# Smaller first and last pairs of node blocks, a fourth place for x, and later loads and statistics in a graph layer on one core

## The chip, the cores and the metric

The kernel runs on one core of one Trainium2 chip. The metric is the device time in microseconds of one execution. Beside the timed runs there is one profiled execution, from which all durations of single instructions come. The core's engines are named as in the profile: PE (matrix multiply; PEld its weight loads), DVE (vector), ACT (scalar and activations), POOL and SP (SP issues most of the transfers, ACT issues those of x). Each engine works through its own instructions in the order in which the program writes them, and waits for the other engines through semaphores.

## The reference

One layer of a graph network over 12,500 nodes of 128 numbers and 412,500 edges of 48 numbers, sorted by the node `dst` that they point to:

```python
h = jnp.maximum(_layernorm(x, axis=-1), 0.0)
agg = jax.ops.segment_sum(edge_attr_48, dst, num_segments=12500)
u = graph_globals[0]                       # the same row for all nodes
cat = jnp.concatenate([h, agg, u], axis=1) # 128 + 48 + 64
hid = jax.nn.relu(cat @ W1 + b1)           # 256
out = x + (hid @ W2 + b2)                  # 128
```

All numbers are float32 (node indices int32).

## The kernel before, in words

**Edges.** The edges are cut into 403 chunks of 1,024, and these into two halves, s = 0 and s = 1, which run side by side on two halves of PE's array. Six chunks of each half form a group (CG = 6), and there are NI = 34 groups. One step of the main loop works on one chunk of each half: `contract` (L321) multiplies eight tiles of edges of each by a one-hot matrix, `oh`, and sums over the group in PSUM (`ps`). A step makes 32 matmul records in the profile, since each float32 matmul leaves two. `onehot` (L311) builds `oh` on DVE one group ahead: half s = 0 at the first step of a group, half s = 1 at its third. `add` (L337) adds the sums of the finished group into `aggT`, once for each half, also at the first step of the next group. Edges lie in a ring of PF = 14 buffers of two chunks each; `next_edges` asks for the next buffer once `contract` is done with one.

**Nodes.** The nodes are cut into 24 blocks of 512 (R = 4 rows on each of 128 partitions), taken in pairs: pair k has one block of each half of the edges, because the sums of both halves grow side by side. 212 nodes in the middle form the last block. For a pair, `normalization` makes eight statistics on DVE (bn_stats, L459), a variance and scale (`variance`, `finish`), and eight normalized rows on ACT (L455). `transpose` (L471) turns a block on PE, and ACT copies it to `hT` (L474). `hidden_x` (L489) multiplies it by the upper part of W1 into `ph`, and adds b2 to x on DVE (`xb`, L485), which is the last use of the block of x. `hidden_sums` (L500) adds the product with `aggT`, and ACT evicts `ph` to `hid` (L508). `output` (L519) makes one row of the result, and `store` adds `xb` (L527) and writes it out through SP (L530).

**Order.** The main loop has 204 steps and three more. In each it writes `contract`, then what `plan` has for the step, the adds and one-hot, waiting stores, one or two parts of the running normalization (`next_part`), and then as many PE pieces of the nodes as a running credit of 0.72 a step allows. The list `pieces` gives each piece the step from which it may run and a price. The sums of pair k may run from the step at which its last group, `ready[k]`, is added; its x parts eight steps sooner. What is left after the last step is written behind it.

**Loads of x.** There are XBUFS = 3 places, each for a pair. `pop_piece` asks for the next pair (`load_x`) when `xb` of the oldest one has been written. The loads are issued by ACT, by `next_x`, at steps given in a list or, at the latest, ahead of the first statistics of that pair:

```python
        if not parts and begun < min(len(pairs), freed + XBUFS):
            normalization(begun)
            begun += 1
        if parts and (force or ...):
            while x_loads and x_loads[0][0] <= parts[0][0]:
                next_x()
            parts.pop(0)[2]()
```

Of the kernel before, what the change touches and what calls it, by code (L numbers as in the profile page):

```python
# [16 lines left out]
P = 128  # L17
# [4 lines left out]
def kernel(  # L22
# [61 lines left out]
    BN = R * P  # L84
    XBUFS = 3
    CL = 2
    PF = 14
    GSTEP = N * GE / E
    LEAST = int(-OFF[0] - SL - 64)


    NP = N // BN // 2
    MID = NP * BN
    NM = N - 2 * NP * BN
    END = MID + NM
    assert NM % R == 0 and NM < BN
    blocks = []
    for k in range(NP):
        blocks += [(k * BN, P), (END + k * BN, P)]
    blocks.append((MID, NM // R))  # L100
    pairs = [[2 * k, 2 * k + 1] for k in range(NP)] + [[2 * NP]]

# [10 lines left out]
    ready = [min(NI - 1, max(  # L113
        int(-(-(blocks[j][0] + BN + PAD + 1 - LEAST - BEGIN[s]) // GSTEP)) - 1
        for s, j in enumerate(pairs[k]))) for k in range(NP)]

# [77 lines left out]

    def rows_of(ap, a, m):

        return ap[a:a + m * R].rearrange("(p r) d -> p (r d)", p=m)

# [3 lines left out]
    def load_x(k):  # L202

        if k >= len(pairs):
            return
        xt = xp.tile([P, 2, R * D], F32, name="xt")

        def load(i, j):
            a, m = blocks[j]
            f = m - m % 16  # L210
            nc.scalar.dma_start(xt[:f, i], rows_of(x, a, f))
            if f < m:
                nc.scalar.dma_start(xt[f:m, i], rows_of(x, a + f * R, m - f))

        for i, j in enumerate(pairs[k]):
            xs[j] = xt[:, i].rearrange("p (r d) -> p r d", d=D)
            x_loads.append((k, lambda i=i, j=j: load(i, j)))

    def next_x():
        if x_loads:  # L220
            x_loads.pop(0)[1]()

# [58 lines left out]
    with nc.allow_non_contiguous_dma(reason="a few hundred numbers, once"):  # L281
# [7 lines left out]
        nc.gpsimd.dma_start(b2_sb, b2[None, :].to_broadcast([P, D]))  # L289

    for k in range(XBUFS):
        load_x(k)
# [132 lines left out]
    def normalization(k):  # L425

        js = pairs[k]
        m = blocks[js[0]][1]
        q = len(js) * R
        st = sp.tile([P, 2 * R, 6], F32, name="st", bufs=2)  # L430
        sc = sp.tile([P, 2 * R], F32, name="sc", bufs=2)
        sh = sp.tile([P, 2 * R], F32, name="sh", bufs=2)
        su = sp.tile([P, 2 * R], F32, name="su")

        def variance():

            me, qe, mo, qo = [st[:m, :q, i] for i in (1, 2, 4, 5)]
            di = sp.tile([P, 2 * R], F32, name="df2")
            va = sp.tile([P, 2 * R], F32, name="va")
            nc.vector.tensor_tensor(di[:m, :q], me, mo, OP.subtract)  # L440
            nc.vector.tensor_tensor(va[:m, :q], qe, qo, OP.add)
            nc.vector.tensor_tensor(su[:m, :q], me, mo, OP.add)
            nc.vector.tensor_tensor(di[:m, :q], di[:m, :q], di[:m, :q], OP.mult)
            nc.vector.scalar_tensor_tensor(va[:m, :q], di[:m, :q], D / 4.0, va[:m, :q], OP.mult, OP.add)  # L444
            nc.scalar.activation(sc[:m, :q], va[:m, :q], AF.Sqrt, bias=eps[:m], scale=1.0 / D)  # L445

        def finish():
            nc.vector.reciprocal(sc[:m, :q], sc[:m, :q])
            nc.vector.scalar_tensor_tensor(sh[:m, :q], su[:m, :q], -0.5, sc[:m, :q], OP.mult, OP.mult)

        def row(i, j, r):
            if r == 0:
                xns[j] = mp.tile([P, R, D], F32, name="xn")
            c = i * R + r
            nc.scalar.activation(xns[j][:m, r], xs[j][:m, r], AF.Relu, bias=sh[:m, c:c + 1], scale=sc[:m, c:c + 1])  # L455

        for i, j in enumerate(js):
            for r in range(R):
                parts.append((k, None, lambda i=i, j=j, r=r: nc.vector.bn_stats(st[:m, i * R + r, :], xs[j][:m, r, :])))  # L459
        parts.append((k, None, variance))  # L460
        parts.append((k, None, finish))
        for i, j in enumerate(js):
            for r in range(R):
                parts.append((k, j, lambda i=i, j=j, r=r: row(i, j, r)))

    def transpose(j):
        m = blocks[j][1]
        pt = pst.tile([P, R, P], F32, name="pt")
        xn = xns.pop(j)
        for r in range(R):  # L470
            nc.tensor.transpose(pt[:, r, :m], xn[:m, r], ident[:m, :m])  # L471

        hT = mp.tile([P, P, R], F32, name="hT", bufs=4)
        nc.scalar.copy(hT[:, :m], pt[:, :, :m].rearrange("d r p -> d p r"))  # L474
        hTs[j] = hT.rearrange("d p r -> d (p r)")

    phs = {}

    def hidden_x(k, a, j):

        m = blocks[j][1]
        if a == 0:
            hids[j] = mp.tile([P, NH, R, P], F32, name="hid", bufs=4)
            xb = mp.tile([P, R, D], F32, name="xb", bufs=3)
            nc.vector.tensor_tensor(xb[:m], xs[j][:m], b2_sb[:m, None, :].to_broadcast([m, R, D]), OP.add)  # L485
            xbs[j] = xb
        phs[j, a] = psh.tile([P, BN], F32, name="ph")
        for c in (0, HI):
            nc.tensor.matmul(phs[j, a][c:c + HI, :R * m], w1h[:, a * P + c:a * P + c + HI], hTs[j][:, :R * m],  # L489
                             start=True, stop=False, skip_group_check=True)  # L490

    def hidden_sums(k, a):

        js = pairs[k]
        if len(js) == 2:
            for s, j in enumerate(js):
                at = blocks[j][0] + shift[s]
                h = slice(s * HI, s * HI + DE)
                for c in (0, HI):
                    nc.tensor.matmul(phs[j, a][c:c + HI], w1a[h, a * P + c:a * P + c + HI], aggT[h, at:at + BN],  # L500
                                     start=False, stop=True, skip_group_check=True)
# [4 lines left out]
        for j in js:  # L506
            m = blocks[j][1]
            nc.scalar.activation(hids[j][:, a, :, :m], phs.pop((j, a))[:, :R * m].rearrange("h (p r) -> h r p", r=R),  # L508
                                 AF.Relu, bias=bias[:, a:a + 1])

    def output(j, r):

        m = blocks[j][1]
        if r == 0:
            pos[j] = pso.tile([P, R, D], F32, name="po")
        for a in range(NH):
            for c in range(0, m, HI):
                k = min(m, c + HI)
                nc.tensor.matmul(pos[j][c:k, r], hids[j][:, a, r, c:k], w2[:, a], start=(a == 0), stop=(a == NH - 1),  # L519
                                 skip_group_check=True)  # L520
        if r == R - 1:
            late.append(j)

    def store(j):
        a0, m = blocks[j]
        ot = mp.tile([P, R, D], F32, name="ot")
        nc.vector.tensor_tensor(ot[:m], pos.pop(j)[:m], xbs.pop(j)[:m], OP.add)  # L527
        k = m - m % 16
        od = ot.rearrange("p r d -> p (r d)")
        nc.sync.dma_start(rows_of(out, a0, k), od[:k])  # L530
        if k < m:
            nc.sync.dma_start(rows_of(out, a0 + k * R, m - k), od[k:m])

# [10 lines left out]
    order = [j for js in pairs for j in js]  # L544
    pieces = [(8 + 3 * j, 0.9, lambda j=j: turn(j)) for j in order[:4]]
    for k, js in enumerate(pairs):
        at = CG * ((ready + [NI - 1])[k] + 1) + 2
        nxt = pairs[k + 2] if k + 2 < len(pairs) else []
        if len(js) == 1:
            pieces.append((at, 0.0, lambda: copy_middle(0)))  # L550
        parts_of = [(at - 8, 0.9, lambda k=k, a=a, j=j: hidden_x(k, a, j)) for a in range(NH) for j in js]
        sums = [(at, 0.9, lambda k=k, a=a: hidden_sums(k, a)) for a in range(NH)]
        m = len(js)
        pieces += parts_of[:m + 1] + sums[:1] + parts_of[m + 1:] + sums[1:]
        for s in range(2):
            if s < len(nxt):
                pieces.append((at, 0.9, lambda j=nxt[s]: turn(j)))
            if s < len(js):
                for r in range(R):
                    pieces.append((at, 0.45, lambda j=js[s], r=r: output(j, r)))  # L560
# [46 lines left out]
    first_nodes(1)  # L607
    next_x()
    next_x()


# [25 lines left out]
    at_step(NI - 1, 3, decide)  # L637
    for step in [4, 7] + list(range(12, CG * NI, 8)):
        at_step(0, step, next_x)

    credit = 0.0
    for step in range(CG * NI + 3):
# [3 lines left out]
        for f in plan.get(step, []):  # L646
            f()
        if k == 0:
            if i > 0:
# [21 lines left out]
    with tc.If(isbad >= 1):  # L671
# [63 lines left out]
        for k, js in enumerate(pairs):  # L735
# [12 lines left out]
            for j in js:  # L748
                for r in range(R):
                    output(j, r)  # L750
# [29 lines left out]
```

## Time and profile before

| | us |
|---|---|
| median of 3 timed runs | 374.79 (373.7 to 376.72) |
| the profiled execution | 374.44 |
| its span | 372.7 |
| busy: PE, PEld | 317.1, 248.3 |
| busy: DVE, ACT | 254.3, 110.0 |
| mean granted clock of PE | 0.943 |
| moved by DMA | 95.35 MB, mean 256 GB/s |

The page counts busy time by engine and cuts the span into 40 slices, in which digits give tenths. A row of a group ends with the idle time of the engine just ahead of that group and what ended most of it. The chain follows the work that ended last back to the start. "Issue" is time in which an engine waited for nothing that the profile shows. A matmul's end is modelled, so a busy PE is not always a fast one; the granted clock, in tenths of full speed on the page, stands beside it for that reason.

### The profile page before, as it was taken

To read this page: it belongs to the slowest core of one execution; us is meant where nothing else is said; L and a number is where in the kernel's file an instruction comes from. 1 tells how busy PE (TensorE), PEld (TensorE's weight loads), DVE (VectorE), ACT (ScalarE), POOL (GpSimd) and SP (SyncE) were. 2 spreads that over 40 slices of the span, in tenths; PEclk is the share of its full clock that TensorE was granted. 3 is DMA by queue.
4 is the path that set the end of the run, shared out by engine and by line. 5 is a ranking of instruction groups with operands and counts; after the bars stand their busy time and mean duration, and the time that the engine had idled before them with its cause. 6 is when DMAs were issued, how large, how long until landed. Compare 5 with 4: busy or idle time off the path is not lost.

```text
span 372.7 us, 17113 instructions
## 1 busy us (share of the span) xinstructions
PE 317.1 (85%) x7787; PEld 248.3 (67%) x7788; DVE 254.3 (68%) x413; ACT 110.0 (30%) x238; POOL 13.1 (4%) x44
## 2 busy tenths in 40 slices
PE   2667599797998998987998999699699898999982
PEld 1566476685785875774696687496397596696551
DVE  4677787876885885765767588695878594884420
ACT  3026406241242231260142341063122440341130
POOL 9400000000000000000000000000000000000000
PEclk9968899999998998899699999999799999999997
DMA  5999799999799899699588877999578979830111
GB/s 187 296 371 369 258 294 329 304 297 320 236 302 306 254 303 321 179 338 313 146 286 276 291 250 228 364 311 355 192 218 274 365 218 322 270 123 33 60 37 42
DMA packets 62812, 95.35 MB, mean 256 GB/s; under 512 B 4385, under 2 KB 55949, under 8 KB 62730
## 3 DMA queue, kind: packets, MB, share of 16 engines
q1 hardware_dynamic: 58864, 87.17, 71.7%
q10 hardware_dynamic: 3578, 6.50, 5.2%
q8 instruction: 63, 1.03, 1.2%
q0 software_dynamic: 288, 0.49, 0.5%
q14 instruction: 19, 0.16, 0.1%
HBM read 87.74 MB, written 6.40 MB: 253 GB/s over the span
## 4 chain that ended last, share of the span: by engine, by line
PE 48%; DVE 23%; DMA 20%; issue 4%; ACT 1%; SPq 1%; DVEq 1%; ACTq 0%
PE ps L321 23%; DMA xt<-in_x_dram 13%; DVE oh L311 13%; PE po L519 8%; DMA e<-in_edge_attr_dram 7%; PE ph L500 6%; PE ph L489 6%; PE pt L471 3%; DVE aggT L337 2%; DVE xb L485 2%; DVE st L459 2%; DVE ot L527 2%; ACT hid L508 1%; DVEq L332 0%; SPq L236 0%
## 5 line engine op out<-in xcount | busy, mean ns | idle before, releaser
L321 PEld LDWEIGHTS ps<-oh,e 128*48 128x48 f32 x6448 | 180.4, 131 | 70.6 <-issue 59.6
L321 PE MATMUL ps<-oh,e 128*48 128x44 f32 x6448 | 189.2, 223 | 16.8 <-issue 10.4
L311 DVE TENSOR_TENSOR oh<-iota,rel 128x2112 f32<-128x2112 f32 (+2 forms) x72 | 157.2, 2205 | 0.9
L508 ACT ACTIVATE hid<-ph,bias 128x512 f32<-128x512 f32 (+1 forms) x50 | 31.2, 671 | 98.2 <-PE ph L500 94.3
L519 PE MATMUL po<-w,hid 128*64 128x128 f32 (+1 forms) x784 | 58.1, 278 | 1.1 <-ACT hid L508 0.6
L489 PE MATMUL ph<-hT,w1h 128*64 128x512 f32 (+1 forms) x200 | 54.7, 624 | 0.8 <-ACT hid L508 0.8
L459 DVE BATCH_NORM_STATS2 st<-xt 128x6 f32<-128x128 f32 (+1 forms) x100 | 23.0, 281 | 46.2 <-DMA xt<-in_x_dram 46.2
L519 PEld LDWEIGHTS po<-w,hid 128*64 128x64 f32 (+1 forms) x784 | 43.4, 137 | 3.0 <-ACT hid L508 2.0
L337 DVE TENSOR_TENSOR aggT<-aggT,ps 48x199 f32 (+1 forms) x68 | 24.3, 357 | 28.8 <-PE ps L321 15.2
L500 PE MATMUL ph<-aggT,w1a 48*64 48x512 f32 x192 | 33.3, 659 | 9.8 <-DVE aggT L337 9.6
L455 ACT ACTIVATE xn<-xt,sh,sc 128x128 f32<-128x128 f32 (+1 forms) x100 | 40.4, 482 | 3.0 <-DMA e<-in_edge_attr_dram 1.5
L474 ACT COPY hT<-pt 128x512 f32<-128x512 f32 (+1 forms) x25 | 14.3, 573 | 45.6 <-PE pt L471 45.6
L527 DVE TENSOR_TENSOR ot<-po,xb 128x512 f32<-128x512 f32 (+1 forms) x25 | 17.3, 691 | 14.0 <-PE po L519 13.4
L471 PE MATMUL pt<-ident,xn 128*128 128x128 f32 (+1 forms) x100 | 17.9, 297 | 5.9 <-ACT xn L455 4.1
L445 ACT ACTIVATE sc<-va,eps 128x8 f32<-128x8 f32 (+1 forms) x13 | 3.9, 300 | 60.0 <-DVE va L444 60.0
L500 PEld LDWEIGHTS ph<-aggT,w1a 48*64 48x64 f32 x192 | 6.9, 135 | 16.1 <-DVE aggT L337 13.3
L471 PEld LDWEIGHTS pt<-ident,xn 128*128 128x128 f32 (+1 forms) x100 | 11.1, 146 | 9.1 <-ACT xn L455 5.1
L485 DVE TENSOR_TENSOR xb<-xt,b_sb 128x512 f32<-128x512 f32 (+1 forms) x25 | 16.3, 682 | 0.0
L489 PEld LDWEIGHTS ph<-hT,w1h 128*64 128x64 f32 x200 | 11.5, 142 | 3.1 <-ACT hid L508 1.7
L387 PE MATMUL pt<-ident,df 108*128 108x108 f32 (+2 forms) x36 | 6.6, 313 | 7.3 <-DVE df L366 7.3
L379 ACT COPY rel<-pt 128x216 f32<-128x216 f32 (+2 forms) x9 | 4.3, 473 | 27.1 <-PE pt L387 27.1
L395 ACT ACTIVATE far<-df,bounds 108x1024 f32<-108x1024 f32 (+2 forms) x10 | 11.5, 1147 | 0.2
(77 smaller groups left out, 63.5 us busy)
## 6 DMA issues: line engine op xcount, KB each, us to landing
e<-in_edge_attr_dram SPq DMA_DIRECT2D x200, 384.0 KB
xt<-in_x_dram ACTq DMA_DIRECT2D x24, 256.0 KB
out_dram<-ot SPq DMA_DIRECT2D x24, 256.0 KB
di<-in_dst_dram SPq DMA_DIRECT2D x6, 216.0 KB
e<-in_edge_attr_dram SPq DMA_DIRECT2D x2, 192.0 KB
di<-in_dst_dram SPq DMA_DIRECT2D x2, 108.0 KB
e<-in_edge_attr_dram SPq DMA_DIRECT2D x1, 159.0 KB
w1h<-in_L_gnn_W_dram POOLq DMA_DIRECT2D x1, 128.0 KB, 6.8
```

The lines of the kernel that those rows point to most:

```text
L311: nc.vector.tensor_tensor(hots[g][:, k0 * T:(k0 + n) * T], iota[:, None, :].to_broadcast([P, n * T, W]), r[:, :, None].to_broadcast([P, n ...
L321: nc.tensor.matmul(ps[s * HI:s * HI + DE, o:o + W], edges[c][0][:, t * DE:(t + 1) * DE], hots[g][:, k * T + t, :], start=(k == 0 and t == ...
L337: nc.vector.tensor_tensor(to, to, acc[i % len(acc)][h, :wg], OP.add)
L455: nc.scalar.activation(xns[j][:m, r], xs[j][:m, r], AF.Relu, bias=sh[:m, c:c + 1], scale=sc[:m, c:c + 1])
L459: parts.append((k, None, lambda i=i, j=j, r=r: nc.vector.bn_stats(st[:m, i * R + r, :], xs[j][:m, r, :])))
L471: nc.tensor.transpose(pt[:, r, :m], xn[:m, r], ident[:m, :m])
L485: nc.vector.tensor_tensor(xb[:m], xs[j][:m], b2_sb[:m, None, :].to_broadcast([m, R, D]), OP.add)
L489: nc.tensor.matmul(phs[j, a][c:c + HI, :R * m], w1h[:, a * P + c:a * P + c + HI], hTs[j][:, :R * m], start=True, stop=False, skip_group_ch ...
L500: nc.tensor.matmul(phs[j, a][c:c + HI], w1a[h, a * P + c:a * P + c + HI], aggT[h, at:at + BN], start=False, stop=True, skip_group_check=True)
L508: nc.scalar.activation(hids[j][:, a, :, :m], phs.pop((j, a))[:, :R * m].rearrange("h (p r) -> h r p", r=R), AF.Relu, bias=bias[:, a:a + 1])
L519: nc.tensor.matmul(pos[j][c:k, r], hids[j][:, a, r, c:k], w2[:, a], start=(a == 0), stop=(a == NH - 1), skip_group_check=True)
L527: nc.vector.tensor_tensor(ot[:m], pos.pop(j)[:m], xbs.pop(j)[:m], OP.add)
```

## The change

- The blocks get sizes of their own. The first two pairs and the last two have blocks of 256 nodes (two rows on each partition), the ten between have 512. There are 14 pairs and the middle, for 12 and the middle before. The sums of a pair, its x part, transposes, statistics and stores follow its size, and so do the prices of its pieces; `ready` too.
- There are four places for x, and 13 edge buffers.
- A load of x remembers the step at which its place came free. `next_x(4)` runs at every third step and issues at most one half of a pair, no sooner than four steps after that. Four halves are issued ahead of the loop.
- The statistics of a pair begin when both halves were issued and the last one at least eight steps ago. A forced part, which a transpose asks for, doesn't wait for this.
- The first four transposes stand at steps 9, 10, 14 and 15 for 8, 11, 14 and 17 before; the last two of them come behind the x parts of pair 0.

```diff
-    XBUFS = 3
+    XBUFS = 4
-    PF = 14
+    PF = 13
-    NP = N // BN // 2
-    MID = NP * BN
-    NM = N - 2 * NP * BN
+    sizes = [2, 2] + [R] * (N // BN // 2 - 2) + [2, 2]
+    NP = len(sizes)
+    MID = sum(sizes) * P
+    NM = N - 2 * MID
...
-    for k in range(NP):
-        blocks += [(k * BN, P), (END + k * BN, P)]
-    blocks.append((MID, NM // R))
+    for k, r in enumerate(sizes):
+        a = sum(sizes[:k]) * P
+        blocks += [(a, P, r), (END + a, P, r)]
+    blocks.append((MID, NM // R, R))
...
-            x_loads.append((k, lambda i=i, j=j: load(i, j)))
-
-    def next_x():
-        if x_loads:
-            x_loads.pop(0)[1]()
+            x_loads.append((k, lambda i=i, j=j: load(i, j), step))
+
+    came = {}
+
+    def next_x(late=0):
+
+        if x_loads and x_loads[0][2] <= step - late:
+            k, load, _ = x_loads.pop(0)
+            load()
+            came[k] = step
...
+    step = -4
     for k in range(XBUFS):
         load_x(k)
...
-    pieces = [(8 + 3 * j, 0.9, lambda j=j: turn(j)) for j in order[:4]]
+    early = [(at, 0.45, lambda j=j: turn(j)) for at, j in zip((9, 10, 14, 15), order)]
+    pieces = early[:2]
...
+        us = 0.9 * blocks[js[0]][2] / R
...
-        pieces += parts_of[:m + 1] + sums[:1] + parts_of[m + 1:] + sums[1:]
+        pieces += parts_of[:m + 1] + (early[2:] if k == 0 else []) + sums[:1] + parts_of[m + 1:] + sums[1:]
...
-        if not parts and begun < min(len(pairs), freed + XBUFS):
+        if not parts and begun < len(pairs) and (force or (
+                begun in came and not any(q == begun for q, _, _ in x_loads) and came[begun] <= step - 8)):
+            while x_loads and x_loads[0][0] <= begun:
+                next_x()
             normalization(begun)
             begun += 1
...
-            while x_loads and x_loads[0][0] <= parts[0][0]:
-                next_x()
             parts.pop(0)[2]()
...
-    next_x()
-    next_x()
+    for _ in range(4):
+        next_x()
...
-    for step in [4, 7] + list(range(12, CG * NI, 8)):
-        at_step(0, step, next_x)
...
             f()
+        if step % 3 == 2:
+            next_x(4)
         if k == 0:
...
+    step += 99
     while pieces:
         pop_piece()
```

More of the change, by code (lines that the diff above doesn't have):

```diff
@@ L113 @@
     ready = [min(NI - 1, max(
-        int(-(-(blocks[j][0] + BN + PAD + 1 - LEAST - BEGIN[s]) // GSTEP)) - 1
+        int(-(-(blocks[j][0] + blocks[j][2] * P + PAD + 1 - LEAST - BEGIN[s]) // GSTEP)) - 1
         for s, j in enumerate(pairs[k]))) for k in range(NP)]
@@ L193, in load_dst, with rows_of @@
         return di
-    def rows_of(ap, a, m):
-        return ap[a:a + m * R].rearrange("(p r) d -> p (r d)", p=m)
+    def rows_of(ap, a, m, r):
+        return ap[a:a + m * r].rearrange("(p r) d -> p (r d)", p=m)
     xs, xns, xbs, hTs, hids, pos = {}, {}, {}, {}, {}, {}
@@ L208, in load @@
         def load(i, j):
-            a, m = blocks[j]
+            a, m, r = blocks[j]
             f = m - m % 16
-            nc.scalar.dma_start(xt[:f, i], rows_of(x, a, f))
+            nc.scalar.dma_start(xt[:f, i, :r * D], rows_of(x, a, f, r))
             if f < m:
-                nc.scalar.dma_start(xt[f:m, i], rows_of(x, a + f * R, m - f))
+                nc.scalar.dma_start(xt[f:m, i, :r * D], rows_of(x, a + f * r, m - f, r))
         for i, j in enumerate(pairs[k]):
             xs[j] = xt[:, i].rearrange("p (r d) -> p r d", d=D)
-            x_loads.append((k, lambda i=i, j=j: load(i, j)))
-    def next_x():
-        if x_loads:
-            x_loads.pop(0)[1]()
+            x_loads.append((k, lambda i=i, j=j: load(i, j), step))
[5 more added lines that the diff above has]
+            came[k] = step
     first = const.tile([1, NG], I32)
@@ L427, in normalization @@
         js = pairs[k]
-        m = blocks[js[0]][1]
-        q = len(js) * R
+        _, m, nr = blocks[js[0]]
+        q = len(js) * nr
         st = sp.tile([P, 2 * R, 6], F32, name="st", bufs=2)
@@ L453, in row @@
                 xns[j] = mp.tile([P, R, D], F32, name="xn")
-            c = i * R + r
+            c = i * nr + r
             nc.scalar.activation(xns[j][:m, r], xs[j][:m, r], AF.Relu, bias=sh[:m, c:c + 1], scale=sc[:m, c:c + 1])
         for i, j in enumerate(js):
-            for r in range(R):
-                parts.append((k, None, lambda i=i, j=j, r=r: nc.vector.bn_stats(st[:m, i * R + r, :], xs[j][:m, r, :])))
+            for r in range(nr):
+                parts.append((k, None, lambda i=i, j=j, r=r: nc.vector.bn_stats(st[:m, i * nr + r, :], xs[j][:m, r, :])))
         parts.append((k, None, variance))
@@ L462, in normalization @@
         for i, j in enumerate(js):
-            for r in range(R):
+            for r in range(nr):
                 parts.append((k, j, lambda i=i, j=j, r=r: row(i, j, r)))
     def transpose(j):
-        m = blocks[j][1]
+        _, m, nr = blocks[j]
         pt = pst.tile([P, R, P], F32, name="pt")
         xn = xns.pop(j)
-        for r in range(R):
+        for r in range(nr):
             nc.tensor.transpose(pt[:, r, :m], xn[:m, r], ident[:m, :m])
-        hT = mp.tile([P, P, R], F32, name="hT", bufs=4)
-        nc.scalar.copy(hT[:, :m], pt[:, :, :m].rearrange("d r p -> d p r"))
-        hTs[j] = hT.rearrange("d p r -> d (p r)")
+        hT = mp.tile([P, BN], F32, name="hT", bufs=4)
+        hTs[j] = hT[:, :m * nr]
+        nc.scalar.copy(hTs[j].rearrange("d (p r) -> d p r", r=nr), pt[:, :nr, :m].rearrange("d r p -> d p r"))
     phs = {}
     def hidden_x(k, a, j):
-        m = blocks[j][1]
+        _, m, nr = blocks[j]
         if a == 0:
@@ L484, in hidden_x @@
             xb = mp.tile([P, R, D], F32, name="xb", bufs=3)
-            nc.vector.tensor_tensor(xb[:m], xs[j][:m], b2_sb[:m, None, :].to_broadcast([m, R, D]), OP.add)
+            nc.vector.tensor_tensor(xb[:m, :nr], xs[j][:m, :nr], b2_sb[:m, None, :].to_broadcast([m, nr, D]), OP.add)
             xbs[j] = xb
@@ L488, in hidden_x @@
         for c in (0, HI):
-            nc.tensor.matmul(phs[j, a][c:c + HI, :R * m], w1h[:, a * P + c:a * P + c + HI], hTs[j][:, :R * m],
+            nc.tensor.matmul(phs[j, a][c:c + HI, :nr * m], w1h[:, a * P + c:a * P + c + HI], hTs[j],
                              start=True, stop=False, skip_group_check=True)
@@ L497, in hidden_sums @@
                 at = blocks[j][0] + shift[s]
+                n = blocks[j][2] * P
                 h = slice(s * HI, s * HI + DE)
                 for c in (0, HI):
-                    nc.tensor.matmul(phs[j, a][c:c + HI], w1a[h, a * P + c:a * P + c + HI], aggT[h, at:at + BN],
+                    nc.tensor.matmul(phs[j, a][c:c + HI, :n], w1a[h, a * P + c:a * P + c + HI], aggT[h, at:at + n],
                                      start=False, stop=True, skip_group_check=True)
@@ L506, in hidden_sums @@
         for j in js:
-            m = blocks[j][1]
-            nc.scalar.activation(hids[j][:, a, :, :m], phs.pop((j, a))[:, :R * m].rearrange("h (p r) -> h r p", r=R),
+            _, m, nr = blocks[j]
+            nc.scalar.activation(hids[j][:, a, :nr, :m], phs.pop((j, a))[:, :nr * m].rearrange("h (p r) -> h r p", r=nr),
                                  AF.Relu, bias=bias[:, a:a + 1])
     def output(j, r):
-        m = blocks[j][1]
+        _, m, nr = blocks[j]
         if r == 0:
@@ L520, in output @@
                                  skip_group_check=True)
-        if r == R - 1:
+        if r == nr - 1:
             late.append(j)
     def store(j):
-        a0, m = blocks[j]
+        a0, m, nr = blocks[j]
         ot = mp.tile([P, R, D], F32, name="ot")
-        nc.vector.tensor_tensor(ot[:m], pos.pop(j)[:m], xbs.pop(j)[:m], OP.add)
+        nc.vector.tensor_tensor(ot[:m, :nr], pos.pop(j)[:m, :nr], xbs.pop(j)[:m, :nr], OP.add)
         k = m - m % 16
-        od = ot.rearrange("p r d -> p (r d)")
-        nc.sync.dma_start(rows_of(out, a0, k), od[:k])
+        od = ot[:, :nr].rearrange("p r d -> p (r d)")
+        nc.sync.dma_start(rows_of(out, a0, k, nr), od[:k])
         if k < m:
-            nc.sync.dma_start(rows_of(out, a0 + k * R, m - k), od[k:m])
+            nc.sync.dma_start(rows_of(out, a0 + k * nr, m - k, nr), od[k:m])
     mid = big.tile([P, NM], F32)
@@ L548 @@
         nxt = pairs[k + 2] if k + 2 < len(pairs) else []
+        us = 0.9 * blocks[js[0]][2] / R
         if len(js) == 1:
             pieces.append((at, 0.0, lambda: copy_middle(0)))
-        parts_of = [(at - 8, 0.9, lambda k=k, a=a, j=j: hidden_x(k, a, j)) for a in range(NH) for j in js]
-        sums = [(at, 0.9, lambda k=k, a=a: hidden_sums(k, a)) for a in range(NH)]
+        parts_of = [(at - 8, us, lambda k=k, a=a, j=j: hidden_x(k, a, j)) for a in range(NH) for j in js]
+        sums = [(at, us, lambda k=k, a=a: hidden_sums(k, a)) for a in range(NH)]
         m = len(js)
-        pieces += parts_of[:m + 1] + sums[:1] + parts_of[m + 1:] + sums[1:]
+        pieces += parts_of[:m + 1] + (early[2:] if k == 0 else []) + sums[:1] + parts_of[m + 1:] + sums[1:]
         for s in range(2):
             if s < len(nxt):
-                pieces.append((at, 0.9, lambda j=nxt[s]: turn(j)))
+                pieces.append((at, 0.9 * blocks[nxt[s]][2] / R, lambda j=nxt[s]: turn(j)))
             if s < len(js):
-                for r in range(R):
+                for r in range(blocks[js[s]][2]):
                     pieces.append((at, 0.45, lambda j=js[s], r=r: output(j, r)))
@@ L748 @@
             for j in js:
-                for r in range(R):
+                for r in range(blocks[j][2]):
                     output(j, r)
```

## The prediction

> **What bounds it now.** I read the page first, then the waits, the chain of waits in order of time, the timeline around one stall, and the windows for the clock.
>
> ```profile
> PE 317.1 (85%) x7787; PEld 248.3 (67%) x7788; DVE 254.3 (68%) x413; ACT 110.0 (30%) x238; POOL 13.1 (4%) x44
> PEclk9968899999998998899699999999799999999997
> DMA  5999799999799899699588877999578979830111
> PE ps L321 23%; DMA xt<-in_x_dram 13%; DVE oh L311 13%; PE po L519 8%; DMA e<-in_edge_attr_dram 7%; PE ph L500 6%; PE ph L489 6%; PE pt L471 3%; DVE aggT L337 2%; DVE xb L485 2%; DVE st L459 2%; DVE ot L527 2%; ACT hid L508 1%; DVEq L332 0%; SPq L236 0%
> L459 DVE BATCH_NORM_STATS2 st<-xt 128x6 f32<-128x128 f32 (+1 forms) x100 | 23.0, 281 | 46.2 <-DMA xt<-in_x_dram 46.2
> ```
>
> No engine is full: PE 85%, DVE 68%, and nearly all of DVE's longest idle time is one row, the statistics waiting for a block of x. The chain puts 13% of the span on that transfer. The waits say how often, and how much reaches PE:
>
> ```profile
> DVE st L459 <- DMA xt<-in_x_dram: 46.2, 13, 6.2
> PE ph L500 <- DVE aggT L337: 9.6, 7, 2.0
> PE ps L321 <- issue: 10.4, 13, 1.7
> PE ps L321 <- DVE oh L311: 6.0, 5, 3.1
> ```
>
> 46.2 us are lost on DVE, thirteen times, but PE loses far less directly. The chain and the timeline of one stall show why:
>
> ```profile
> 133.22 4.63 DVE oh L311 x2
> 137.87 0.69 DVE ot L527
> 138.56 1.21 DVE xb L485 x2
> 139.80 4.33 DMA xt<-in_x_dram
> 145.16 2.54 PE ph L500 x8
> ```
> ```profile
> 144.15 0.68 DVE L459 BATCH_NORM_STATS2 st<-xt 128x6 f32<-128x128 f32 x3 [4.38 <-DMA xt<-in_x_dram]
> 144.75 0.35 DVE L337 TENSOR_TENSOR aggT<-aggT,ps 48x199 f32 x1
> 145.16 2.54 PE L500 MATMUL ph<-aggT,w1a 48*64 48x512 f32 x8 [1.65 <-DVE aggT L337]
> ```
> ```profile
> 143.00:144.00 1.00, 0.51 (x23) 0.39 (x17) 0.00 (x0) 0.00 (x0) 0.00 (x0) 1.00 1.07 402
> 145.00:146.00 1.00, 0.84 (x6) 0.46 (x8) 0.77 (x3) 0.00 (x0) 0.00 (x0) 0.81 1.08 382
> 146.00:147.00 1.00, 1.00 (x6) 0.02 (x2) 1.00 (x1) 0.24 (x1) 0.00 (x0) 0.50 1.07 371
> ```
>
> The last xb (L485) frees a place of x; ACT issues the next load at once (139.80); the next instruction in DVE's order is the first bn_stats of that very pair. DVE stands still for 4.38 us, the add of sums into aggT (L337) stands behind it, and PE, which works on from its lead, then waits 1.65 us for that add. Then the granted clock is 0.50 (third number from the end of a window). So a DVE stall of about 4.5 us costs PE a gap of 1 to 3 us and some microseconds at half clock.
>
> **Part 1: the x wait goes.** With four pairs on the chip, a load no sooner than four steps after its place came free, and statistics no sooner than eight steps after the load was issued. Following the order that both loops write out: before, loads of pairs 4 to 11 and their first bn_stats stand in the same step (40, 58, 76, 94, ...); after, the second half of pairs 5, 7, 9 goes out in steps 35, 65, 101 and the statistics begin in steps 47, 76, 111. The least distance is 8 steps; in undisturbed stretches six steps take 8 to 9 us (starts of steps 90, 96 at 164, 173 us; 126, 132 at 225, 233), so at least 11 us, against 6.2 us for the longest wait. I take all waits on xt as gone. What PE gets:
> - PE's gaps behind the late aggT or one-hot tile, each following an x wait: 1.96 (at 88.3), 1.20 (116.6), 1.65 (145.2), 1.90 (175.6), 1.84 (238.1), 3.12 and 0.50 (264.5, 266.0), 0.54 (317.1): **12.7 us**.
> - Time lost to the clock, as 1 minus the granted clock summed over two-microsecond windows: 118 to 122: 1.7; 144 to 154: 3.4; 176 to 184: 3.4; 264 to 272: 3.4: **11.9 us**. All four lie just behind such a gap.
>
> Here the Trainium skill speaks against the gain. "TensorE: Matmul & The Clock Gate", section "HAM oscillation", gives the rule of no idle gaps above about 3.4 us. All gaps here are shorter (1.20 to 3.12), so by the rule the four stretches would have another cause and stay: gain 12.7 only. By the rows, half clock follows gaps of 1.20, 1.65, 1.90 and 3.12 (though not those of 1.96 and 1.84), and no half clock appears between 50 and 345 us without such a gap. I take the row: 24.6 us. Keeping the clock loss is rival B.
>
> Cross-check by steps, from the count of weight loads of L321: steps 12 to 198 run from 37 to 340 us, 31 groups of six. Eight groups with a costly x wait take 100 us, the other 23 take 203, or 8.8 each. 8 x (12.5 - 8.8) = 29.6, less some 4 us of "issue" gaps lying in those eight: about 25.6. It agrees.
>
> **Part 2: what is late next.** PE's order then meets two things. In pairs 4 and later a sum matmul (L500) sometimes stands in the step of an add or the one after: the add takes 0.74 us for both halves and 0.2 to start, one step of 32 matmul records covers 0.71, so 0.2 to 0.5 us, some five times: +1.5 (between 0 and 4, if DVE's own order runs later). The pace of 8.6 us for six steps compares with DVE's 4.63 for one-hots, 0.74 for adds and at most about 3 of others, so DVE follows narrowly. "Issue" gaps, 10.4 us, fall where the DMA share is 1.0 or more; the bytes are the same in less time, but the bursts behind stalls shrink: between -5 and +5, I take 0.
>
> **Part 3: small pairs at the start.** Pair 0 is ready at group 2 instead of 3, its first hidden matmuls stand in step 12 instead of 18. The statistics wait at 36.8 (2.37 us) goes, and with it part of PE's 4.12 us at 43.1 and of 1.7 us of half clock. But until 42 us DMA runs at 350 to 387 GB/s, four x loads of the new places (pairs 2, 3) are issued there, and in step 31 pair 3 is transposed before its rows are normalized: finish, four activations of 0.48, some 2.5 us. Between -5 and +4, taken **-1.5**. Total work does not shrink: two pairs more bring twelve or so small DVE instructions each (0.16 to 0.2) and a fixed part of about 0.15 for each extra xb and ot (199 columns of L337 take 0.357, 106 take 0.26): some 3.5 us of DVE over the run. Where DVE has slack that is free; without it 3.5. Taken **+1**.
>
> **Part 4: small pairs at the end.** The last contraction ends near 345.2, the last output matmul at 365.35. What PE has behind it now: sums of pair 10, 1.09; a transpose, 0.45; 16 groups of outputs of pairs 10 and 11 at 0.44, 7.0; x part and sums of pair 11, 3.5 and 2.1; middle 3.7; with the transpose of L410, 18.1. Afterwards: outputs of pair 11, 3.5; two transposes, 0.8; pairs 12 and 13 at 1.76 + 1.05 + 1.76 each (four x parts and four outputs of 0.44, the x parts at half of the 0.88 shown for 512 columns, sums at half of 2.1), 9.1; middle 3.7, L410: 17.3. Before, it waits 0.78 + 0.41 + 0.24 for hid there; the smaller pairs wait about twice 0.5 + 0.2 and 0.24. Net 18.9 for 19.5, **-0.6**: the pairs are smaller, but the small ones all run behind the edges; the end hardly shrinks.
>
> **Part 5: one edge buffer less, four x places.** Each buffer holds two chunks and a step uses two, so the lead falls from 14 steps to 13, some 19 us at the new pace. SP waited 160.6 us for PE to free buffers, PE waited for edges under 1 us, so one step less is free; 0 to 3, taken 0. Needed rate: after 46 us some 80 MB in about 260 us, 310 GB/s, against 350 to 400 shown when it is full. The extra x and store issues (0.33 and 0.36 us each) lie in idle time of ACT and SP.
>
> **Sum** against the profiled execution's 374.4 (span 372.7): -12.7 -11.9 +1.5 -1.5 +1 -0.6 = -24.2, or **350**. The median shown, 374.8, is 0.4 above it; I leave that.
>
> **Rivals.**
> - **B, 361 (357 to 369):** DVE is on time, but gaps of about 1 us remain behind adds or "issue", and the half clock stays. Gain 12.7 + 0.6, no start: 361. For it: the skill's rule, and gaps without clock loss at 88 and 238, so the link is loose. Against: every clock loss follows an x gap.
> - **C, 341:** the bursts behind DVE's stalls also caused most "issue" gaps (67.8, 74.0, 162.1, 312.2 lie where DMA is over 1.0): 5 more, and 4 more at the start.
> - **D, slower, 386:** x loads now stand on ACT directly ahead of the evictions of hid (steps 44, 47, 62, 65, 80, 83, ...), where before they stood beside xb. If an issue has to wait, hid is late, ph does not come free, and the next x part (0.7 us later) stalls PE. The one such wait shown is 1.5 us (xn held at 30.3 until an edge load). 24 half loads x 1.5 = 36: 374.4 - 24.2 + 36 = 386. It decides from 1.0 us a load. Against: ACT waits 94.3 us for PE ahead of those evictions (up to 12.2), so an issue has that time, and its places came free four steps earlier.
> - **E, no change, 373:** PE's gaps come back behind other DVE work, because DVE is near its own pace. Against: 23 groups already run at 8.8.
>
> **Chances.** Forecast (343 to 357) 0.52, B 0.20, C 0.10, E 0.05, D 0.13. This measurement can tell about 1% from no change. Faster: 0.82; same: 0.05; slower: 0.13. The range 339 to 367 takes in the forecast, most of B and C, and the clock term.
>
> **What would show it.** Right: st waits for xt under 5 us, xt off the chain, L500's waits for aggT under 3 us, no half clock between 50 and 330 us, last contraction ending near 322, and about 19 us from there to the last output matmul. Wrong: idle time of hid, xn or hT put down to DMA on ACT (D); PE waiting for e (part 5); clock rows of 0.5 behind gaps of 1 us (B); six-step groups above 9.5 us with no x wait (E).

## The result, and the profile after

The changed kernel took 358.75 us (median of 4 runs, 355.26 to 362.1) where the kernel before took 375.75 in the same comparison: a ratio of 0.953, with an interval of 0.942 to 0.965. Timed again beside the last experiments it took 358.59, ratio 0.955 (0.947 to 0.963). The forecast was 350, with 339 to 367 around it: the direction and the mechanism held, the gain was 17 us between the medians and 14.8 between the profiled executions, where 24 were expected. The profiled execution took 359.69, its span is 357.9. Some executions took over 1.5% longer than the fastest of their kernel; the ratios and intervals leave these out, and where too few others were left for an interval, only times are given.

From the page of the changed kernel: engine rows, clock, DMA, the chain by line and the statistics (L468 now, L459 before):

```profile
PE 309.5 (86%) x7851; PEld 248.5 (69%) x7852; DVE 255.9 (71%) x435; ACT 113.1 (32%) x252; POOL 13.1 (4%) x44
PEclk9986988989999999899999999989998999999997
DMA  5999984899987999999899889989989699930110
PE ps L330 37%; PE po L529 13%; PE ph L498 11%; DVE oh L320 7%; PE ph L510 6%; PE pt L480 4%; DMA di<-in_dst_dram 3%; DMA e<-in_edge_attr_dram 2%; PE pt L396 1%; DVE aggT L346 1%; DVE st L468 1%; SPq L149 1%; ACT xn L464 1%; ACT hid L518 1%; DVE df L375 1%
L468 DVE BATCH_NORM_STATS2 st<-xt 128x6 f32<-128x128 f32 (+1 forms) x100 | 23.1, 279 | 0.0
```

The 46.2 us ahead of the statistics are 0.0, and xt, 13% of the chain before, is gone from it. The chain is now a chain of PE: its contraction (L330) went from 23% to 37%. No engine is much busier. What took the place of the wait is seen in PE's waits (engine, tile and line, what it waited for, us in total, times, longest):

```profile
PE ps L330 <- issue: 8.3, 8, 2.2
PE ph L498 <- ACT hid L518: 7.5, 5, 4.7
PE ps L330 <- DVE oh L320: 3.2, 4, 1.4
PE ph L510 <- issue: 2.1, 1, 2.1
PE po L529 <- issue: 1.7, 2, 1.3
```

The sums of a pair (now L510) no longer wait for aggT (9.6 us before, no row now). The gaps put down to issue are 12.1 us in these three rows; before, they were 10.4 in the row of the sums over edges (`ps`) and 0.6 in two smaller ones. New is the wait of the x part (L498) for an eviction of hid, 4.7 us of it at one place at the start.

Where the 15 us came from is read from the step at which the loop stands, counted from the weight loads of the contraction (to 1 us):

| | before | after |
|---|---|---|
| step 36 begins | 76 | 82 |
| step 198 begins | 340 | 325 |
| between them | 264 | 243 |
| last contraction to last output matmul | 20.1 | 20.3 |

**The middle gained 21, the start lost 6, the end is as long as it was.** The windows over the middle close the sum (busy time and count of PE, PEld, DVE, ACT, POOL, then granted clock, DMA share and GB/s; before, then after):

```profile
76.00:340.00 264.00, 240.94 (x6165) 189.36 (x6161) 192.16 (x280) 77.22 (x167) 0.42 (x1) 0.95 0.83 269
```
```profile
82.00:325.00 243.00, 230.10 (x6143) 184.16 (x6140) 194.01 (x299) 75.00 (x165) 0.42 (x1) 0.98 0.89 293
```

PE's idle time falls from 23.1 to 12.9 us: 12.7 behind x and 1.4 of smaller gaps went, 3.9 of issue came. Its busy time falls by 10.8, of which the clock can explain at most 6.8 (11.9 us lost before, 5.1 after). Most of the other 4.0 was also waiting for aggT, inside groups that the profile counts as busy: a group of eight sums stands for both halves, and the second half waited for its own add. Before, a group and the weight load of its second half; after, a group:

```profile
88.31 1.65 PE L500 MATMUL ph<-aggT,w1a 48*64 48x512 f32 x8 [1.96 <-DVE aggT L337]
88.88 0.19 PEld L500 LDWEIGHTS ph<-aggT,w1a 48*64 48x64 f32 x4 [0.38 <-DVE aggT L337]
```
```profile
120.21 1.09 PE L510 MATMUL ph<-aggT,w1a 48*64 48x512 f32 x8
```

Five such groups took 1.54 to 1.65 us before, at the full clock or nearly so, where the others took 1.09: 2.7 us together.

### The profile page after: what moved, and what is told of

Same layout as the page of the kernel before. It is cut to its first block, busy times and chain, and to the rows that moved or that the text cites. A ratio compares the mean times of both kernels' runs of the same rounds, so it can differ in the third digit from the quotient of the medians.

```text
span 357.9 us, 17292 instructions
## 1 busy us (share of the span) xinstructions
PE 309.5 (86%) x7851; PEld 248.5 (69%) x7852; DVE 255.9 (71%) x435; ACT 113.1 (32%) x252; POOL 13.1 (4%) x44
## 2 busy tenths in 40 slices
DMA packets 63964, 95.35 MB, mean 266 GB/s; under 512 B 4513, under 2 KB 58125, under 8 KB 63882
## 3 DMA queue, kind: packets, MB, share of 16 engines
q8 instruction: 63, 1.03, 1.2%
## 4 chain that ended last, share of the span: by engine, by line
PE 71%; DVE 12%; issue 6%; DMA 5%; ACT 3%; SPq 2%; DVEq 0%; ACTq 0%
PE ps L330 37%; PE po L529 13%; PE ph L498 11%; DVE oh L320 7%; PE ph L510 6%; PE pt L480 4%; DMA di<-in_dst_dram 3%; DMA e<-in_edge_attr_dram 2%; PE pt L396 1%; DVE aggT L346 1%; DVE st L468 1%; SPq L149 1%; ACT xn L464 1%; ACT hid L518 1%; DVE df L375 1%
## 5 line engine op out<-in xcount | busy, mean ns | idle before, releaser
L330 PEld LDWEIGHTS ps<-oh,e 128*48 128x48 f32 x6448 | 178.6, 130 | 60.9 <-issue 52.3
L330 PE MATMUL ps<-oh,e 128*48 128x44 f32 x6448 | 187.3, 222 | 11.8 <-issue 8.3
L498 PE MATMUL ph<-hT,w1h 128*64 128x512 f32 (+2 forms) x232 | 53.5, 547 | 7.6 <-ACT hid L518 7.5
L346 DVE TENSOR_TENSOR aggT<-aggT,ps 48x199 f32 (+1 forms) x68 | 24.3, 357 | 47.7 <-PE ps L330 24.6
L518 ACT ACTIVATE hid<-ph,bias 128x512 f32<-128x512 f32 (+2 forms) x58 | 32.7, 614 | 73.7 <-PE ph L510 71.1
L484 ACT COPY hT<-pt 128x512 f32<-128x512 f32 (+2 forms) x29 | 15.0, 517 | 55.4 <-PE pt L480 55.4
L537 DVE TENSOR_TENSOR ot<-po,xb 128x512 f32<-128x512 f32 (+2 forms) x29 | 17.9, 616 | 18.6 <-PE po L529 18.0
L510 PE MATMUL ph<-aggT,w1a 48*64 48x512 f32 (+1 forms) x224 | 27.8, 565 | 2.1 <-issue 2.1
L454 ACT ACTIVATE sc<-va,eps 128x8 f32<-128x8 f32 (+2 forms) x15 | 4.5, 298 | 66.2 <-DVE va L453 66.2
L468 DVE BATCH_NORM_STATS2 st<-xt 128x6 f32<-128x128 f32 (+1 forms) x100 | 23.1, 279 | 0.0
L498 PEld LDWEIGHTS ph<-hT,w1h 128*64 128x64 f32 x232 | 13.1, 138 | 10.9 <-ACT hid L518 9.4
L494 DVE TENSOR_TENSOR xb<-xt,b_sb 128x512 f32<-128x512 f32 (+2 forms) x29 | 16.9, 606 | 0.0
```

Source lines behind the costliest of these rows:

```text
L330: nc.tensor.matmul(ps[s * HI:s * HI + DE, o:o + W], edges[c][0][:, t * DE:(t + 1) * DE], hots[g][:, k * T + t, :], start=(k == 0 and t == ...
L346: nc.vector.tensor_tensor(to, to, acc[i % len(acc)][h, :wg], OP.add)
L494: nc.vector.tensor_tensor(xb[:m, :nr], xs[j][:m, :nr], b2_sb[:m, None, :].to_broadcast([m, nr, D]), OP.add)
L498: nc.tensor.matmul(phs[j, a][c:c + HI, :nr * m], w1h[:, a * P + c:a * P + c + HI], hTs[j], start=True, stop=False, skip_group_check=True)
L510: nc.tensor.matmul(phs[j, a][c:c + HI, :n], w1a[h, a * P + c:a * P + c + HI], aggT[h, at:at + n], start=False, stop=True, skip_group_check ...
L518: nc.scalar.activation(hids[j][:, a, :nr, :m], phs.pop((j, a))[:, :nr * m].rearrange("h (p r) -> h r p", r=nr), AF.Relu, bias=bias[:, a:a ...
```

## The experiments

Ratios are to the kernel before, from the same rounds. An expectation names its views "Theory A", "Theory B" and so on; the text behind it takes them up by these names.

### Which part makes the gain

**All pairs of 512**, the handling of x as changed:

```diff
-    sizes = [2, 2] + [R] * (N // BN // 2 - 2) + [2, 2]
+    sizes = [R] * (N // BN // 2)
...
-    early = [(at, 0.45, lambda j=j: turn(j)) for at, j in zip((9, 10, 14, 15), order)]
-    pieces = early[:2]
+    early = [(8 + 3 * j, 0.9, lambda j=j: turn(j)) for j in order[:4]]
+    pieces = early[:4]
...
```

> The changed kernel with all pairs of 512 nodes and the first transposes of before; the four places, 13 edge buffers, late loads and late statistics stay. Theory A: the gain is the x wait alone, and the small pairs at the start cost about 6 us (step 36 begins at 82 us after the change and at 76 before it), because evictions of hid stand on ACT behind normalization that waits for DVE. Then this kernel is 5 to 7 us faster than the changed one, about 352 to 354, and step 36 begins near 76. Theory B: the start is late because four x loads share DMA with the first edges; then this kernel is as slow at the start and takes 358 to 360.

Measured: 361.95 us, ratio 0.957 (0.949 to 0.965). Step 36 begins at 85. Theory A, that small pairs at the start cost 6 us, fails: without them the start is later still. The time lies nearer to Theory B's 358 to 360, but its cause, four x loads that share DMA with the first edges, is not what makes the changed kernel's start late: the run without the distance (below) has the same loads, and its step 36 begins at 76.

**Small pairs at the start only**, and **at the end only** (`sizes = [2, 2] + [R] * 11`; `[R] * 11 + [2, 2]`, the latter with the first transposes of before):

> The changed kernel with small pairs at the start only; the last two small pairs become one of 512. Theory A (the small end brings nothing: last contraction to last output matmul is 20.3 us after the change, 20.1 before): same as the changed kernel within 1 us, 358 to 359.5. Rival: the small end brings the 2 to 4 us that a half-sized last pair would have by its own length; then 361 to 362.

> The changed kernel with small pairs at the end only, first transposes as before the change. Theory A: like all pairs of 512, about 352 to 354, step 36 near 76 us. Theory B: 358 to 360, step 36 near 82.

Measured: 359.33 us for the first (354.5 to 362.85); 361.74, ratio 0.963 (0.954 to 0.972), for the second, with step 36 at 80. These three and the changed kernel (0.953 and 0.955) can't be told apart by their times. With the distance in place, the small pairs are worth less than can be measured at either end.

**The small pairs alone**, with before's three places, 14 edge buffers and order of loads:

```diff
-    XBUFS = 4
-    PF = 13
+    XBUFS = 3
+    PF = 14
...
-        if not parts and begun < len(pairs) and (force or (
-                begun in came and not any(q == begun for q, _, _ in x_loads) and came[begun] <= step - 8)):
-            while x_loads and x_loads[0][0] <= begun:
-                next_x()
+        if not parts and begun < min(len(pairs), freed + XBUFS):
...
+            while x_loads and x_loads[0][0] <= parts[0][0]:
+                next_x()
             parts.pop(0)[2]()
...
-    for _ in range(4):
+    for _ in range(2):
         next_x()
...
-        if step % 3 == 2:
-            next_x(4)
+        if step in (4, 7) or step >= 12 and step % 8 == 4:
+            next_x()
```

> Before's handling of x (three places, 14 edge buffers, loads at before's steps and ahead of the first statistics) with the small pairs at both ends. Theory A: the x waits return in the middle (some 10 of about 4 us) and the start is late: 6 us over before, about 380. Theory B: no more than before, 373 to 376. A third view, that the small pairs bring the gain: about 360.

Measured: 396.78 us, ratio 1.041 (1.029 to 1.054). The wait is back, with 61.0 us in a profiled execution of 398.69, where the kernel before has 46.2 in one of 374.44:

```profile
DVE st L468 <- DMA xt<-in_x_dram: 61.0, 17, 7.5
```

So the gain is that of the handling of x as a whole; with before's handling, small pairs cost 4%.

### The place or the distance

**Three places**, the late loads and late statistics kept (`XBUFS = 4` to `3`):

> The changed kernel with three places of x; late loads and late statistics stay. Following the order: statistics still begin eight steps behind the second half of their load in the middle (load in steps 47, 65, 83, statistics in steps 55, 73, 91), but pairs 3 and 4 are forced in steps 31 and 48, and the middle block in the tail. Theory P (the fourth place makes the gain): x waits come back, 370 or more. Theory Q (the distance between load and statistics makes it, places only help at the ends): no x wait in the middle, 5 to 9 us lost at the start and 3 in the tail, 364 to 371, with steps 60 to 190 as fast as in the changed kernel (8.9 to 9.2 us for six).

Measured: 380.77 us (374.9 to 390.18). The fastest execution, which is the profiled one, took 374.9; the fastest of the kernel before in these rounds took 370.19. There is no gain at all, yet the statistics wait for xt nowhere. Theory Q is right that the distance alone removes the x wait, and wrong on where that costs: steps 36 to 198 take 253 us for 243 in the changed kernel, 10 of the 15 us between the two. PE's waits show what came in its place:

```profile
PE ph L498 <- ACT hid L518: 13.3, 9, 4.7
PE pt L480 <- ACT xn L464: 10.7, 6, 3.7
```

Loads come one pair later, statistics eight steps behind them, so rows are normalized just ahead of their transposes, or forced, and stand on ACT ahead of evictions of hid. The wait for x was turned into a wait for rows and hid. The fourth place gives the time in which the distance costs nothing: following the order, with three places the statistics of pairs 3 and later begin exactly eight steps behind their load, held there by the rule, and with four those of pairs 4 to 12 begin nine to fifteen steps behind it, held by nothing.

**No distance**, with four places:

```diff
-                begun in came and not any(q == begun for q, _, _ in x_loads) and came[begun] <= step - 8)):
+                begun in came and not any(q == begun for q, _, _ in x_loads) and came[begun] <= step)):
```

> The changed kernel with statistics as soon as the load was issued, in place of eight steps behind. Following the order, steps 32 to 176 are written exactly as in the changed kernel, since with four places the load is 11 to 12 steps ahead there anyway; at the start the statistics begin in step 0, the scale of pair 2 comes ahead of the one-hot of step 18 and pair 3 isn't forced in step 31. Theory R (the distance of eight steps binds only at the start, where it costs): st waits for xt once or twice at the start, no x wait later, step 36 at 76 to 79 in place of 82, and up to 6 us faster, 352 to 358, less what the gaps put down to issue take back. Theory S (the distance is what removes the x wait): x waits come back in the middle, 365 or more.

Measured: 352.29 us (351.34 to 355.32), ratio 0.938 (0.930 to 0.945), against 0.955 (0.947 to 0.963) for the changed kernel in the same rounds: faster than both kernels, and the two intervals don't overlap. Theory R holds: x is waited for once, at the start, and nowhere later:

```profile
DVE st L468 <- DMA xt<-in_x_dram: 4.6, 1, 4.6
```

Step 36 begins at 76; from there to step 198 it takes 245 us, for 243 in the changed kernel. Following the order, the edit changes what is written in steps 0 to 31 and in four steps from 177 to 181, nothing else; the lead that it keeps is made at the start.

Why, is read from the timeline of the start, of which the rows that matter stand here. In the changed kernel (start, duration, engine and line; the idle time before it in brackets):

```profile
47.19 0.70 PE L510 MATMUL ph<-aggT,w1a 48*64 48x256 f32 x8
47.21 2.36 DVE L320 TENSOR_TENSOR oh<-iota,rel 128x2112 f32<-128x2112 f32 x1
49.93 0.17 DVE L453 SCALAR_TENSOR_TENSOR va<-df,va 128x8 f32<-128x8 f32 x1
50.70 0.17 DVE L458 SCALAR_TENSOR_TENSOR sh<-su,sc 128x8 f32<-128x8 f32 x1
50.95 0.49 ACT L464 ACTIVATE xn<-xt,sh,sc 128x128 f32<-128x128 f32 x1 [0.52 <-DVE sh L458]
52.12 0.81 ACT L518 ACTIVATE hid<-ph,bias 128x256 f32<-128x256 f32 x2
52.63 1.12 PE L498 MATMUL ph<-hT,w1h 128*64 128x256 f32 x4 [4.74 <-ACT hid L518]
```

PE has the first sums of pair 0 done before 48 us. Their eviction stands on ACT behind the scale and rows of pair 2; these wait for DVE, where the scale stands behind a one-hot of 2.36 us. The three ph tiles are full, and PE waits 4.74 us; from 50 to 57 us the clock is at half, 3.4 us more. Waits of 1.32 and 1.11 us for hid and rows follow at 68.9 and 72.8, with another 1.7 us lost to the clock from 74 to 78. Without the distance:

```profile
47.41 0.17 DVE L453 SCALAR_TENSOR_TENSOR va<-df,va 128x8 f32<-128x8 f32 x1
48.18 0.17 DVE L458 SCALAR_TENSOR_TENSOR sh<-su,sc 128x8 f32<-128x8 f32 x1
49.67 4.63 DVE L320 TENSOR_TENSOR oh<-iota,rel 128x2112 f32<-128x2112 f32 x2
50.37 0.81 ACT L518 ACTIVATE hid<-ph,bias 128x256 f32<-128x256 f32 x2
50.88 0.65 PE L498 MATMUL ph<-hT,w1h 128*64 128x256 f32 x4 [0.53 <-ACT hid L518]
```

The scale is ahead of the one-hot, the eviction follows the sums, PE waits 0.53 us, and no half clock appears from 40 to 76 us. Four steps' delay of the first statistics (step 4 for 0) had pushed pair 2's scale behind a one-hot.

**Faster parts at the start**, the other way to that order:

```diff
-        for _ in range(2 if step % 2 or step < 20 else 1):
+        for _ in range(3 if 14 <= step < 18 else 2 if step % 2 or step < 32 else 1):
```

> The changed kernel with three parts of the normalization a step in steps 14 to 17 and two in every step up to 31. Then the scale of pair 2 is made ahead of the one-hot of step 18 and not behind it, pair 3 is not forced in step 31, and the evictions of pair 0 don't stand on ACT behind rows that wait for DVE. If that order costs the start, the gap of 4.74 us at 52.6 (waiting for hid) and the half clock behind it go, step 36 begins near 74 to 76 in place of 82, and the time falls by 5 to 8 us to 351 to 354. If the start is bound by DMA, the gap moves to another place and it stays at 357 to 360.

Measured: 358.46 us (351.98 to 359.52). Three executions took 358.3 to 359.52; the fourth took 351.98, which is what was expected if the order costs the start. As a time it is inconclusive. In the profiled execution, one of the three, step 36 begins at 76 as expected and the gap of 4.74 is 1.70, but half clock stays from 49 to 57, and step 198 begins at 324, no more than 1 us ahead of the changed kernel. Whether the fast one also gave its lead back is not shown. For the order at the start the run agrees.

**First loads by POOL**, with all pairs of 512:

```diff
+        q = nc.gpsimd if k < XBUFS else nc.scalar
...
-            nc.scalar.dma_start(xt[:f, i, :r * D], rows_of(x, a, f, r))
+            q.dma_start(xt[:f, i, :r * D], rows_of(x, a, f, r))
...
```

> The kernel with all pairs of 512, in which the loads of the first four pairs are issued by POOL and not by ACT. In the equal-pair kernel PE waited 7.56 and 5.80 us for normalized rows at 33.6 and 49.2 us, while ACT stood behind its own x loads. If ACT is held by those loads (rival D of the prediction, at the start only), both gaps fall below 4 us, step 36 begins at 76 to 79 in place of 85, and the time falls by 5 to 8 us, to 354 to 357. If the gaps come from x landing late, DVE or PE wait for xt instead and the time stays at 360 to 363.

Measured: 354.65 us, ratio 0.949 (0.937 to 0.961), which overlaps that of equal pairs with loads by ACT. The two gaps of PE ahead of transposes stay, 7.42 and 5.78 us for 7.56 and 5.80, so ACT's x loads don't make them, and rival D's mechanism is not what costs the start. That late statistics make them here too is argued from the order (step 4 for 0, a transpose in step 8); equal pairs without the distance were not run.

### The gaps put down to issue

**Half of the edge bytes.** Half of the edges is left out; the number of instructions stays:

```diff
-                e[:, :f], edge_attr[c0 * CE:(c0 + f) * CE].rearrange("(c p t) d -> p c (t d)", p=P, t=T))
+                e[:, :f, :T * DE // 2],
+                edge_attr[c0 * CE:(c0 + f) * CE].rearrange("(c p t) d -> p c (t d)", p=P, t=T)[:, :, :T * DE // 2])
...
-                    ps[s * HI:s * HI + DE, o:o + W], edges[c][0][:, t * DE:(t + 1) * DE],
+                    ps[s * HI:s * HI + DE, o:o + W], edges[c][0][:, t % (T // 2) * DE:(t % (T // 2) + 1) * DE],
```

> The changed kernel loads only the first half of every full chunk's rows and multiplies those twice: half of the edges is left out, instructions and their number stay, edge bytes are halved. Theory F: PE's gaps put down to issue are instructions that come late while DMA is full; then they fall from about 12 us to under 3, the half clock behind them goes, and the start, bound by DMA until 42 us, is earlier: 335 to 345. Theory G: those gaps have nothing to do with DMA; they stay at 8 to 14 us and the time at 350 to 358.

Measured: 338.81 us (338.42 to 339.28), ratio 0.908 (0.899 to 0.916). Steps 36 to 198 take 226 us for 243. The windows over them, and PE's wait:

```profile
78.00:304.00 226.00, 224.28 (x6185) 179.23 (x6182) 194.37 (x301) 75.64 (x165) 0.42 (x1) 1.00 0.62 180
```
```profile
PE ps L331 <- issue: 0.5, 1, 0.5
```

PE is idle 1.7 us in 226, the clock is full, and the issue gaps are 0.5 us. The number of DMA packets is the same (63,964), only their bytes fell, from 95.35 to 55.83 MB. So the load of DMA in bytes makes these gaps, and with it some 17 us of the middle. That instructions come late is theory F's reading; the profile has a queue of 1.03 MB of instructions, but shows no single fetch behind a gap, so this step is inferred.

**Stores by POOL**, so that SP asks for edges without standing behind stores (`nc.sync` to `nc.gpsimd` in `store`):

> The changed kernel with the stores issued by POOL, so that SP, which asks for edges, no longer stands behind stores that wait for DVE (41.1 us in 17 waits). If the gaps put down to issue (about 12 us after the change, 0.5 with half of the edge bytes) come from bursts of edge loads behind those waits, they fall to under 6 us and the time by 6 to 10, to 349 to 353. If they come from the mean load of DMA (0.89 of its time in steps 36 to 198), they stay within 9 to 14 and the time at 356 to 360.

Measured: 360.68 us, ratio 0.950 (0.939 to 0.961), and

```profile
PE ps L330 <- issue: 11.2, 13, 2.8
```

The gaps stay, though SP no longer waits for stores in the loop: bursts behind SP's store waits are not their cause.

**All three together**, no distance, stores and first loads by POOL:

> No distance, stores from POOL, and the loads of the first four pairs from POOL. If the start gains 5 and the bursts 6, 347 to 350. If the load of DMA sets the middle, a start that is 5 us earlier is partly given back in issue gaps, as with the faster parts (start 6 us earlier, time 0 to 1 us shorter): 354 to 358.

Measured: 357.0 us, ratio 0.948 (0.938 to 0.957). No more than the distance alone brings. In its profiled execution of 359.93 us PE waits 8.45 us for df, the second block of dst, at 23.8 (6.86 without the other two edits); the loads by POOL alone don't explain that, since with them the equal pairs wait 2.7 there. Why the three together bring no more stays open. The changed kernel again, in the same rounds:

> The changed kernel itself, timed beside the kernel before in the same rounds as the next three: 0.945 to 0.965 of before, 355 to 362.

Measured: 358.59 us (357.07 to 360.05), as expected.

## Why the prediction was right, and where it was off

The time lies inside the range of 339 to 367, but outside the forecast's own band of 343 to 357 and inside that of rival B. Of the signs named, the first three came, and so did the 19 us at the end (20.3). Half clock between 50 and 330 us did not stay away, and the last contraction ended near 330 and not 322.

**Part 1, the x wait goes:** right. All 46.2 us are gone, and so are the 12.7 us of PE's gaps behind them. The reason given was half right: after, the load is nine to fifteen steps ahead for pairs 4 to 12 because of the fourth place, and the eight-step rule binds at the start and, by one step, at pair 13.

**Part 1, the clock:** mis-sized, and not the same in each execution. The step that failed is "I take the row: 24.6 us", 11.9 of it clock. In the profiled execution half clock still takes 5.1 us of the middle, so at most 6.8 came back. Half clock follows other gaps too; the windows at one of issue, of the changed kernel:

```profile
228.00:230.00 2.00, 0.28 (x13) 0.28 (x14) 2.00 (x2) 1.22 (x3) 0.00 (x0) 1.00 1.06 390
230.00:232.00 2.00, 2.00 (x55) 1.78 (x50) 0.27 (x2) 0.59 (x1) 0.00 (x0) 0.79 1.06 378
232.00:234.00 2.00, 2.00 (x34) 2.00 (x32) 0.00 (x0) 0.00 (x0) 0.00 (x0) 0.50 0.78 262
```

A gap of 2.22 us to 229.7, DMA at 1.06, then the clock at 0.50. The same follows issue gaps of 1.73 (148.5) and 2.08 (274.7), 1.7 us each time. But the second profiled execution of the same kernel has a gap of 2.28 us at the same matmul, to 229.75, and none of it:

```profile
231.00:232.00 1.00, 1.00 (x37) 0.83 (x37) 0.00 (x0) 0.59 (x1) 0.00 (x0) 1.00 1.05 339
232.00:233.00 1.00, 1.00 (x30) 1.00 (x26) 0.00 (x0) 0.00 (x0) 0.00 (x0) 1.00 1.02 342
```

There the middle (82 to 324 us) lost 1.7 us to the clock. The row was still nearer than the rule of no gaps above 3.4 us, in the Trainium skill's "TensorE: Matmul & The Clock Gate", section "HAM oscillation": by it none of the 11.9 would have come back, and the longest gap of the middle, 3.12 us before and 2.22 after, stays below that length although half clock came. But the link is not to x alone, and the length of the gap does not decide; what does stays open.

**Part 2, what is late next:** the waits behind adds (taken +1.5) did not appear. Issue gaps, taken 0 between -5 and +5, rose by 3.9 in the middle, inside their ends, and the half clock behind them took 5.1 more, which the sum didn't carry. For the middle the parts said about -22 with the added DVE work; it gave -21. That these agree to 1 us is luck: the 9 us of issue gaps and clock that were missed are nearly made up by 4.0 of busy time (2.7 of it the waits inside the groups of sums) and 1.4 of smaller gaps, which the sum didn't have, and by 2.5 for adds and DVE work, which did not show.

**Part 3, the start:** the step that failed with the largest miss. Taken -1.5 with ends at -5 and +4, it came to +6, outside its ends. The working priced the forced transpose in step 31 (2.5 us; it showed 1.1) and missed that normalization put four steps later moves pair 2's scale behind a one-hot, and the eviction of hid behind both: a gap of 4.74 and 3.4 of half clock. With that order undone, in the run without the distance, step 36 is back at 76. The order had been followed by steps and not along ACT's and DVE's own queues.

**Part 4, the end:** right in substance, -0.6 said, +0.2 found; the small pairs do run behind the edges.

**Part 5, one edge buffer less:** PE's wait for edges on matmuls did not grow to a row; nothing in the runs speaks against the 0, though the buffer was not varied alone.

The misses, 7.5 at the start, 1 in the middle and 0.8 at the end, make 9.3 of the 9.5 us between 350.2 and 359.7. **Rival B** had the nearest time (361), and its point, that half clock stays behind gaps of issue, is in part what happened; its claim that no gain comes at the start was too mild. **Rival D** did not occur in the middle: ACT still waits 71.1 us for PE ahead of evictions. **E** failed with the middle. **C** had the sign of the issue gaps wrong.

## What to carry to other kernels

When a wait is moved away by delaying work, follow the delayed work in each engine's own order: an eight-step distance that costs nothing where a spare buffer already gives nine steps or more cost some 6 us at the start, where it bound. A spare buffer and a later consumer are two edits. Here the buffer carried the gain: three places with the same distance gained nothing, and four without it gained most. Three places without it were not run; in their written order the statistics of pairs 4 and later stand in the step of their load, as before the change. Nor was the number of places changed with before's steps of loading kept. Price a stall removed on PE twice, by its gap and by the clock behind it, and give the clock part a wide range: two executions of one kernel lost 5.1 and 1.7 us to it in the same stretch.

## What the runs showed of the hardware

The load of DMA acts on PE without any wait for data that the profile shows: at a DMA share of 0.89 and 293 GB/s PE lost about 12 us to issue gaps, at 0.62 and 180 GB/s 0.5 us, with the same number of instructions and of DMA packets. Half clock in the middle came in stretches of some 3.4 or 7 us, with 1.7 or 3.4 us lost, and in these executions no length of gap tells when: it followed gaps of 1.20, 1.65 and 1.90 us before the change, and of 1.73, 2.08 and 2.22 after it; gaps of 1.84 and 1.96 before, and of 2.28 in the second execution after it, went without.
